# Second block of a two-block transformer: how the normalised rows get turned before each projection

## The chip, the core and the metric

One core of a Trainium2 chip runs the whole program in one launch. TensorE (PE) multiplies matrices into PSUM, VectorE (DVE), ScalarE (ACT) and GpSimd (POOL) work on SBUF and, but for POOL, on PSUM, and SyncE (SP) issues most DMAs. Each engine works off its own queue in order; they meet at semaphores. The metric is the device time of one execution in microseconds (us). Everything is float32.

## The reference, cut to what matters

Eight sequences of 512 rows of 256 numbers pass through two blocks, one after the other. The second block, which the change is about, does this for each sequence (16 heads of 64; context of 64 rows):

```
adaln(x, w, b) = ln(x) * w' + b'          # w', b': one vector of 256 per sequence
x = attn(adaln(x, 1), adaln(x, 1), sa) + x     # rotary self-attention, 512 x 512 scores
x = attn(adaln(x, 1), ln(context),  ca) + x     # rotary cross-attention, 512 x 64 scores
x = gelu(adaln(x, 2) @ ff_w1 + b1) @ ff_w2 + b2 + x     # hidden width 1024
```

`ln` subtracts a row's mean and divides by its standard deviation. The three `adaln` results feed the projections; a projection needs its input with the 256 features on partitions, while `ln` needs the rows on partitions. So 3 x 8 = 24 tiles of 512 x 256 have to be turned in this block.

## The kernel before, in words

**Tiles.** Each sequence's `x` stays in SBUF as a tile of 128 partitions x 4 x 256 (row t*128+p). A norm is made in three pieces (`norm_pieces`, lines 173-195): two of statistics, and `apply`, which writes the normed rows `z` with four DVE instructions (L191). `z` has one buffer in the pool `nk`, so the next sequence's `z` waits until this one has been read. POOL's `add_row` (L427) then adds an output bias to `x`.

**The turn.** `transposed` (lines 400-408) turns `z` with 8 PE transposes of 128 x 128 (L406) into two PSUM banks; ACT then writes the feature-major tile `hT`, scaled and shifted per feature (L407). `pair_turned` (lines 953-962) is the same in the self-attention stage, with one PSUM pair (L959, L961). `hT` has one buffer in each of the pools `nk` and `wk`.

**Stages.** Block 1 runs first (0 to about 804 us of the span). At its end `first_norm` and `first_turn` (lines 891-901) prepare the second block's first tile. Then follow self-attention (`slots`, to about 1758 us), cross-attention (`cross`, lines 1350-1393, to about 2093 us with the first feed-forward pieces in it) and feed-forward.

- Self-attention, per sequence four groups `g` of four heads. The next sequence's norm pieces stand in groups 0 and 1, its turn as the last job in the middle of group 2; group 3 makes its first queries, keys and values. `sums`, `sums_back`, `inverse` and `inverse_back` send the softmax sums through DRAM to spread them over partitions: den to DRAM, back as rec, reciprocal on DVE, to DRAM, back as `rb`, each broadcast to 64 partitions. The pool `wk` has two buffers with the tag `t`; the two rotary products and the values `v` for the next stage use them.
- Cross-attention, per sequence eight steps `j`. Queries run `LEAD` = 6 steps ahead, so sequence b+1 needs its `hT` at step j=2 of sequence b. Its rows are normed in the sequence before that, at j=5, 6 and 7 (`rows_`, `apply` at j=7, where it stands behind the residual addition of `cross_out`), and turned at j=1 (`turn`). The sums take the same way through DRAM: `sums` at j=0 (of the sequence before) and j=4, `inverse` at j=1 and j=6, with eight `rb` DMAs each.
- Feed-forward, per sequence `up` (f32 128 x 512 matmuls into hidden rows, gelu on ACT), the turn of the next sequence, and `down`, with the norm of the one after that in its middle.

**Order.** The order of instructions on PE, DVE, ACT and POOL is the program's own, by `manual_schedule` around each stage (lines 265, 1183, 1417). SP is not in these lists: the order of SP's DMAs is chosen by the tile framework's scheduler. All loads, the sums' DMAs and the output go by SP; the last sums of self-attention go by ACT's queue (`queue`, L1046). Waits on SP hold up all DMAs behind them.

Of the kernel before, what the change touches and what calls it, by code (L numbers as in the profile page):

```python
# [10 lines left out]
F32 = mybir.dt.float32  # L11
I32 = mybir.dt.int32
AF = mybir.ActivationFunctionType
ALU = mybir.AluOpType
AX = mybir.AxisListType
ENG = mybir.EngineType

B, N, D, H, T, CD, FF = 8, 512, 256, 16, 64, 192, 1024
P = 128
NT = N // P  # L20
EPS0, EPS1 = 1e-6, 1e-5
# [23 lines left out]
def fast_path(ctx: ExitStack, tc: tile.TileContext, a: dict, out: bass.AP):  # L45

    nc = tc.nc
# [4 lines left out]
    dram = ctx.enter_context(tc.tile_pool(name="dram", bufs=2, space=bass.MemoryType.DRAM))  # L52
# [10 lines left out]
    def pair():  # L63
        return psum.tile([P, 2, 512], F32, tag="pair", name="ps_P", bufs=4)
# [26 lines left out]
    ident = const.tile([P, P], F32, name="ident")  # L91
# [27 lines left out]
    def row(name):  # L119
        lo, hi = _ROWS[name]  # L120
        return rows[:, lo:hi]
# [27 lines left out]
    a1 = const.tile([P, 2, B], F32, name="a1")  # L149
    b1 = const.tile([P, 2, B], F32, name="b1")  # L150
# [59 lines left out]
    wk = sa0.enter_context(tc.tile_pool(name="sa0", bufs=2, side="right"))  # L210
# [51 lines left out]

    first_mod = bank_x()
    ms = ExitStack()
    ms.enter_context(tc.manual_schedule(engines={ENG.PE, ENG.DVE, ENG.Activation, ENG.Pool}))
    nc.sync.dma_start(cT, a["cT"].rearrange("(k p) b -> p k b", p=P))
    for k in range(2):
        nc.scalar.dma_start(adaw[:, k, 0 : 2 * D], a["adaln_wT"][k * P : (k + 1) * P, 0 : 2 * D])
# [131 lines left out]
    def transposed(pool, z, b, am, bm, bufs=2):  # L400

        hT = pool.tile([P, 2, N], F32, tag="hT", name="hT", bufs=bufs)
        for k in range(2):
            ps = bank_x()
            for t in range(NT):
                nc.tensor.transpose(ps[:, t * P : (t + 1) * P], z[:, t, k * P : (k + 1) * P], ident)  # L406
            nc.scalar.activation(hT[:, k, :], ps, AF.Identity, bias=bm[:, k, b : b + 1], scale=am[:, k, b : b + 1])  # L407
        return hT

    def normed_in_pieces(pool, b, eps, take):  # L410

        def rows_():
            z = pool.tile([P, NT, D], F32, tag="z", name="z", bufs=1)
            take(z)
            return z

        return norm_pieces(rows_, xs[b], eps)


    def normed(pool, b, eps):  # L420
        z = pool.tile([P, NT, D], F32, tag="z", name="z", bufs=1)
        layernorm(z, xs[b], eps)
        return z

    def add_row(b, r):

        nc.gpsimd.tensor_tensor(xs[b], xs[b], r[:, None, :].to_broadcast([P, NT, D]), ALU.add)  # L427
# [462 lines left out]

    def first_turn():
        nonlocal ready
        ready = transposed(nk, ready, 0, a1, b1, 1)

    def first_norm(n):
        nonlocal ready
        if n == 0:
            first.extend(normed_in_pieces(nk, 0, EPS1, first.append))
        first[n]()
        if n == 2:  # L900
            ready = first[-1]

    first = []
    beginning()
# [43 lines left out]
    with tc.tile_pool(name="ph4", bufs=2, reuse_waits="tile") as wk:  # L948
        NG = H // 4
        kb, vb = kv_first()  # L950
        first_rows, ahead = [], []

        def pair_turned(z, b):

            hT = nk.tile([P, 2, N], F32, tag="hT", name="hT", bufs=1)
            ps = pair()
            for k in range(2):
                for t in range(NT):
                    nc.tensor.transpose(ps[:, k, t * P : (t + 1) * P], z[:, t, k * P : (k + 1) * P], ident)  # L959
            for k in range(2):  # L960
                nc.scalar.activation(hT[:, k, :], ps[:, k, :], AF.Identity, bias=b1[:, k, b : b + 1], scale=a1[:, k, b : b + 1])  # L961
            return hT

        class Batch:

# [5 lines left out]
            def norm(self, n):  # L971
                self.pieces[n]()
                if n == 2:
                    add_row(self.b, row("sabo"))

            def turn(self):
                self.s["hT"] = pair_turned(self.s["z"], self.b)

            def values(self, half, t0):
                s = self.s  # L980
# [128 lines left out]
        def slots():  # L1109
            first = todo[0]  # L1110
            first.s["hT"] = ready
            second = pair()
            first.queries(0)
            add_row(0, row("sabo"))
            first.turned(0, w_sk, "k", second, nc.vector)
            first.values(0, 0)
            first.values(0, 2)
            before = None
            for b, this in enumerate(todo):
                nxt = todo[b + 1] if b + 1 < B else None  # L1120
                last = todo[b - 1] if b else None
                for g in range(NG):
                    for kt in range(2):
                        this.score(g, kt)
                    this.add(g, 1)
                    if g < NG - 1:
                        jobs = [lambda: this.queries(g + 1), lambda: this.keys(g + 1)]
                        if g == 1 and last:
                            jobs.append(last.out)
                        if b:  # L1130
                            jobs.append(lambda: this.values((g + 1) // 2, 2 * (1 - g % 2)))
                        elif g < 2:
                            jobs.append(lambda: this.values(1, 2 * g))
                        if g == 2 and nxt:
                            jobs.append(nxt.turn)
                    elif nxt:
                        jobs = [lambda: nxt.queries(0), lambda: nxt.keys(0), lambda: nxt.values(0, 0)]
                    else:
                        jobs = [lambda: cross_values(wk, 0)]
                    for n, fn in enumerate(jobs):  # L1140
                        fn()
                        if n == 0 and before:
                            before[0].inverse(before[1])
                        if n == 0 and nxt and g == 0:
                            nxt.norm(0)
                    if b == B - 1 and g == 2:
                        cross_weights()
                    if b == 0 and g == 1:
                        nc.gpsimd.memset(vb, 0.0)
                        load_kb(0)  # L1150
                    for kt in (2, 3):
                        this.score(g, kt)
                        this.add(g, kt)
                    this.value(g)
                    if nxt and g < 2:
                        nxt.norm(g + 1)
                    if before:
                        before[0].scaled(before[1])
                    this.sums(g)
                    before = this, g  # L1160
            end = todo[-1]
            first_rows.append(normed(nk, 0, EPS1))
            add_row(0, row("cabo"))
            cross_values(wk, 1)
            end.sums_back(NG - 1)
            cross_values(wk, 2)
            end.s["ps"] = [half[:, i, 0:D] for half in (pair(), pair()) for i in range(2)]
            end.inverse(NG - 1)
            cross_values(wk, 3)
            end.inverse_back(NG - 1)  # L1170
            load_vb(0)
            end.last_out(range(6))
            end.scaled(NG - 1)
            first_rows.append(pair_turned(first_rows[0], 0))
            end.last_out((6, 7))
            first_rows.append(normed(nk, 1, EPS1))
            add_row(1, row("cabo"))

            ahead.extend(normed_in_pieces(nk, 2, EPS1, lambda z: turned_rows.update({2: z})))
            ahead[0]()  # L1180
            ahead[1]()

        with tc.manual_schedule(engines={ENG.PE, ENG.DVE, ENG.Activation, ENG.Pool}):
            slots()
    other_banks()

    w_co, w_cq, ready = cross["o"], cross["q"], first_rows[1]
# [4 lines left out]
    with tc.tile_pool(name="ph5", bufs=2, reuse_waits="tile") as wk:  # L1192
# [3 lines left out]


        turned_rows = {0: ready, 1: first_rows[2]}

        pieces = {2: [lambda: None, lambda: None, ahead[2]]}  # L1200

        def rows_(i, n=None):

            if i < 2 * B:
                b = i % B
                if not n and i not in pieces:
                    pieces[i] = normed_in_pieces(nk, b, EPS1, lambda z: turned_rows.update({i: z}))
                for piece in pieces[i] if n is None else pieces[i][n : n + 1]:
                    piece()
                if n in (None, 2):  # L1210
                    add_row(b, row("ffb2" if i // B else "cabo"))

        def turn(i):
            if i < 2 * B:
                am, bm = ((a1, b1), (a2, b2))[i // B]
                turned_rows[i] = transposed((nk, wk)[i % 2], turned_rows[i], i % B, am, bm, 1)

        ss = [{} for _ in range(B)]

# [194 lines left out]
                    good = within(top)  # L1414
            return good

        with tc.manual_schedule(engines={ENG.PE, ENG.DVE, ENG.Activation, ENG.Pool}):
            cross()
            return feed_forward()

# [861 lines left out]
```

## Time and profile before

| | |
|---|---|
| runs | 2298.50, 2303.84, 2307.77 us, median 2303.84 |
| profiled execution | 2300.09 us, of which the span (first to last instruction) 2298.0 us |
| mean granted TensorE clock | 0.997 |
| all PE transposes of `transposed` (L406), 256 of them | 20.6 + 10.1 + 3.6 + 3.0 us busy |
| PE transposes of `pair_turned` (L959), 64 | 8.3 us busy |
| DMA engines | 10.7% of their time on SP's queue, 79 MB moved in all |

A timeline line reads: start in us of the span, length in us, engine, line of the kernel, operation, written tile <- read tiles, shapes, count of merged instructions; in brackets the idle time ahead of it and what ended that. A line of the chain of work reads: start, length, engine, tile written, line, count. Of a merged run of matmuls the length includes the last one's drain, so the next run starts a little before it ends. SP's lines show how long the issuing of a DMA took, not when it landed.

### The profile page before, as it was taken

What the parts mean: (1) busy time and instruction counts of PE and PEld (TensorE: products, weight loads), DVE (VectorE), ACT (ScalarE), POOL (GpSimd) and SP (SyncE); (2) the same over time, 40 slices, a digit from 0 to 9 for tenths busy, and PEclk for the clock granted to TensorE, in tenths of its full rate; (3) what the DMA queues carried; (4) which work ended last, traced back from release to release, by engine and by line L of the source; (5) the groups of instructions that cost most, each with busy time, mean ns of one, the idle gap of its engine ahead of it and who ended that gap; (6) DMA issues with size and microseconds to landing.
All of it is one profiled execution on the core that took longest, in us unless ns stands there. A gap on an engine that the chain in (4) does not pass through costs nothing.

```text
span 2298.0 us, 31044 instructions
## 1 busy us (share of the span) xinstructions
PE 2278.0 (99%) x12372; PEld 1169.5 (51%) x12372; DVE 1076.0 (47%) x1911; ACT 865.9 (38%) x1309; POOL 920.9 (40%) x584
## 2 busy tenths in 40 slices
PE   9999999999999999999999999999999999999999
PEld 4444554544545643535353444444445556567666
DVE  5676565565555345353444444444434554532110
ACT  5665555455542134342424333333332222231221
POOL 4653333333200046464545555554544544431110
PEclk9999999999999999999999999999999999999999
DMA  6120000000002000000000000000123222221000
GB/s 197 47 84 5 13 7 6 12 6 3 3 1 90 0 10 20 20 20 20 20 20 20 20 20 20 12 28 11 29 61 108 75 76 67 67 62 34 19 19 20
DMA packets 76697, 78.99 MB, mean 34 GB/s; under 512 B 37264, under 2 KB 54400, under 8 KB 76544
## 3 DMA queue, kind: packets, MB, share of 16 engines
q1 hardware_dynamic: 75064, 73.75, 10.7%
q8 instruction: 100, 1.64, 0.3%
q0 software_dynamic: 576, 2.10, 0.2%
q10 hardware_dynamic: 904, 1.07, 0.1%
q14 instruction: 53, 0.43, 0.1%
HBM read 67.38 MB, written 9.51 MB: 33 GB/s over the span
## 4 chain that ended last, share of the span: by engine, by line
PE 96%; DVE 2%; POOL 1%; issue 1%; ACT 0%; POOLq 0%; DVEq 0%; ACTq 0%
PE ps_P L88 41%; PE ps_B L88 30%; PE ps_X L88 7%; PE ps_S L88 6%; PE ps_D L88 5%; PE ps_O L88 4%; PE ps_B L545 1%; PE ps_B L406 1%; POOL var L536 1%; PE ps_B L577 1%; PE ps_X L406 0%; PE ps_P L959 0%; DVE z L191 0%; POOL rstd L158 0%; DVE st L182 0%
## 5 line engine op out<-in xcount | busy, mean ns | idle before, releaser
L594 ACT ACTIVATE p<-ps_B 128x512 f32<-128x512 f32 x576 | 292.6, 626 | 163.6 <-PE ps_B L88 163.5
L1020 ACT ACTIVATE p<-ps_P 128x1024 f32<-128x1024 f32 x256 | 245.1, 1027 | 95.1 <-PE ps_P L88 95.1
L88 PE MATMUL ps_P<-q,k 32*128 32x512 f32 x2048 | 239.1, 600 | 0.5 <-DVE t L999 0.5
L1029 POOL TENSOR_TENSOR sm<-sm,p 128x1024 f32<-128x1024 f32 x64 | 174.9, 2732 | 139.3 <-ACT p L1020 139.2
L88 PE MATMUL ps_B<-hT,w 128*128 128x512 f32 x512 | 226.6, 597 | 0.6 <-ACT hT L407 0.4
L88 PE MATMUL ps_P<-p,v 128*32 128x512 f32 x2048 | 226.4, 594 | 0.0
L158 POOL TENSOR_TENSOR rstd<-rstd,mhalf 128x4 f32<-128x4 f32 x49 | 52.0, 1062 | 325.7 <-DVE rstd L157 324.7
L988 ACT COPY v<-ps_P 128x1024 f32<-128x1024 f32 x32 | 32.4, 1013 | 377.0 <-PE ps_P L88 377.0
L1029 DVE TENSOR_TENSOR sm<-sm,p 128x1024 f32<-128x1024 f32 x64 | 98.5, 1538 | 150.3 <-ACT p L1020 150.3
L88 PEld LDWEIGHTS ps_P<-q,k 32*128 32x128 f32 x2048 | 101.1, 184 | 132.3 <-issue 104.5
L88 PEld LDWEIGHTS ps_B<-hT,w 128*128 128x128 f32 x512 | 95.4, 190 | 126.2 <-issue 99.9
L88 PEld LDWEIGHTS ps_P<-p,v 128*32 128x32 f32 x2048 | 63.3, 110 | 158.3 <-issue 134.8
L1027 POOL TENSOR_TENSOR sm<-p 128x1024 f32<-128x1024 f32 x32 | 79.2, 2474 | 160.6 <-ACT p L1020 160.6
L88 PE MATMUL ps_B<-q,k 16*128 16x512 f32 x1024 | 140.2, 617 | 1.4 <-DVE k L549 1.4
L536 POOL TENSOR_TENSOR var<-var,mhalf 128x32 f32<-128x32 f32 (+1 forms) x17 | 87.9, 5173 | 104.8 <-DVE var L530 104.8
L998 DVE TENSOR_TENSOR t<-ps_P,rope_c 128x1024 f32<-128x1024 f32 x64 | 78.4, 1225 | 107.9 <-POOL q L1002 66.2
L1027 DVE TENSOR_TENSOR sm<-p 128x1024 f32<-128x1024 f32 x32 | 39.2, 1226 | 185.7 <-ACT p L1020 185.7
L88 PE MATMUL ps_P<-hT,w_sa_wq 128*128 128x512 f32 x256 | 118.4, 605 | 0.8 <-DVE tmp L450 0.8
L88 PE MATMUL ps_B<-p,h 128*32 128x512 f32 x1024 | 117.1, 595 | 0.0
L588 POOL TENSOR_TENSOR attn<-attn,gate 128x256 f32<-128x256 f32 x32 | 23.6, 736 | 230.0 <-DVE attn L586 229.0
L88 PE MATMUL ps_B<-w,hid 128*128 128x256 f32 x512 | 115.4, 385 | 0.0
L88 PE MATMUL ps_P<-hT,w_sa_wk 128*128 128x512 f32 x256 | 115.1, 592 | 0.0
(260 smaller groups left out, 3716.5 us busy)
## 6 DMA issues: line engine op xcount, KB each, us to landing
rb<-rec SPq DMA_DIRECT2D x128, 128.0 KB
rb<-rec_d SPq DMA_DIRECT2D x124, 128.0 KB
out_dram<-x SPq DMA_DIRECT2D x15, 256.0 KB
x<-in_x_dram SPq DMA_DIRECT2D x7, 512.0 KB
gate<-modd SPq DMA_DIRECT2D x24, 128.0 KB
k_d<-q POOLq DMA_DIRECT2D x4, 512.0 KB, 4.0
v_d<-v SPq DMA_DIRECT2D x4, 512.0 KB
w_ff_w<-in_ff_w_dram SPq DMA_DIRECT2D x2, 1024.0 KB
```

The lines of the kernel that those rows point to most:

```text
L88: nc.tensor.matmul(o, lhsT, rhs, start=start, stop=stop)
L158: nc.gpsimd.tensor_tensor(r[:, :n], r[:, :n], mhalf[:, :n], ALU.pow)
L406: nc.tensor.transpose(ps[:, t * P : (t + 1) * P], z[:, t, k * P : (k + 1) * P], ident)
L536: nc.gpsimd.tensor_tensor(var, var, half, ALU.pow)
L545: nc.tensor.transpose(ps[:, t * P : (t + 1) * P], zs[c][:, t, lo : lo + P], ident)
L588: nc.gpsimd.tensor_tensor(attn, attn, gate.to_broadcast([P, NT, 4, HD0]), ALU.mult)
L594: nc.scalar.activation(p[i], ps, AF.Exp, scale=HD0 ** -0.5)
L988: nc.scalar.copy(s["v", half][:, t0 : t0 + 2, :], ps)
L998: nc.vector.tensor_tensor(c, ps, rope_c[:, None, :].to_broadcast([P, 2, N]), ALU.mult)
L1020: nc.scalar.activation(pr, pss[u], AF.Exp, scale=HD1 ** -0.5)
L1027: eng.tensor_tensor(s["sm", g, u], s["p", g, 0, u], s["p", g, 1, u], ALU.add)
L1029: eng.tensor_tensor(s["sm", g, u], s["sm", g, u], s["p", g, kt, u], ALU.add)
```

## The change

The second block's turns no longer use TensorE. DVE turns `z` in blocks of 32 x 32 (one instruction over 128 x 1024), four DMAs write the blocks to a DRAM tile in the order of the features, one DMA reads them back into the buffer of `z`, and ACT scales and shifts from SBUF into `hT`. The DMAs and the block-turn are issued right after `apply`, ahead of `add_row`; ACT's instructions stand where the turn stood. In the self-attention stage the block-turned copy takes a buffer of the tag `t`; elsewhere it takes the coming `hT` tile itself. SP joins the engines in program order, in all three stages. Block 1's turns stay as they were.

```diff
+    def blocks_turned(by_way, z):
+
+        flat_, zf = by_way.rearrange("p k n -> p (k n)"), z.rearrange("p t d -> p (t d)")
+        nc.vector.transpose(flat_.rearrange("p (q t i) -> p t q i", q=8, t=NT), z.rearrange("p t (q j) -> p t q j", j=32))
+        d = dram.tile([4, 32, 2, 4, P], F32, tag="turned", name="turned_d")
+        for r in range(4):
+            nc.sync.dma_start(d[:, :, :, r, :].rearrange("a j k c -> j k a c"),
+                              flat_[32 * r : 32 * r + 32].rearrange("j (k a c) -> j k a c", k=2, a=4))
+        nc.sync.dma_start(zf, d.rearrange("a j k r c -> (a j) (k r c)"))
+        return zf.rearrange("p (k r t i) -> p k t r i", k=2, r=4, t=NT)
+
+    def modulated(hT, raw, b, am, bm):
+
+        for k in range(2):
+            nc.scalar.activation(hT[:, k, :].rearrange("p (t r i) -> p t r i", t=NT, r=4), raw[:, k], AF.Identity,
+                                 bias=bm[:, k, b : b + 1], scale=am[:, k, b : b + 1])
+        return hT
...
     def first_turn():
         nonlocal ready
-        ready = transposed(nk, ready, 0, a1, b1, 1)
+        ready = modulated(first[-1], ready, 0, a1, b1)
...
         if n == 2:
-            ready = first[-1]
+            z = first[-1]
+            first.append(rows_tile(nk))
+            ready = blocks_turned(first[-1], z)
...
                 if n == 2:
+                    self.s["raw"] = blocks_turned(by_way(), self.s["z"])
                     add_row(self.b, row("sabo"))
 
             def turn(self):
-                self.s["hT"] = pair_turned(self.s["z"], self.b)
+                self.s["hT"] = modulated(rows_tile(nk), self.s["raw"], self.b, a1, b1)
...
-            first_rows.append(normed(nk, 0, EPS1))
+            first_rows.append(blocks_turned(by_way(), normed(nk, 0, EPS1)))
             add_row(0, row("cabo"))
...
-            first_rows.append(pair_turned(first_rows[0], 0))
+            first_rows.append(modulated(rows_tile(nk), first_rows[0], 0, a1, b1))
             end.last_out((6, 7))
-            first_rows.append(normed(nk, 1, EPS1))
+            first_rows.append(blocks_turned(by_way(), normed(nk, 1, EPS1)))
...
                 if n in (None, 2):
+                    row_tiles[i] = rows_tile((nk, wk)[i % 2])
+                    turned_rows[i] = blocks_turned(row_tiles[i], turned_rows[i])
                     add_row(b, row("ffb2" if i // B else "cabo"))
...
-                turned_rows[i] = transposed((nk, wk)[i % 2], turned_rows[i], i % B, am, bm, 1)
+                turned_rows[i] = modulated(row_tiles.pop(i), turned_rows[i], i % B, am, bm)
...
-        with tc.manual_schedule(engines={ENG.PE, ENG.DVE, ENG.Activation, ENG.Pool}):
+        with tc.manual_schedule(engines={ENG.PE, ENG.DVE, ENG.Activation, ENG.Pool, ENG.SP}):
```

`rows_tile(pool)` allocates a tile `hT` as before, and `by_way()` a tile `t` of the self-attention stage. The last hunk stands for three places: ENG.SP is added to each `manual_schedule`. The four outgoing DMAs carry 128 KB each in runs of 512 bytes, the one back 512 KB in runs of 4 KB.

More of the change, by code (lines that the diff above doesn't have):

```diff
@@ L264, in fast_path @@
     ms = ExitStack()
-    ms.enter_context(tc.manual_schedule(engines={ENG.PE, ENG.DVE, ENG.Activation, ENG.Pool}))
+    ms.enter_context(tc.manual_schedule(engines={ENG.PE, ENG.DVE, ENG.Activation, ENG.Pool, ENG.SP}))
     nc.sync.dma_start(cT, a["cT"].rearrange("(k p) b -> p k b", p=P))
@@ L407, in transposed, with rows_tile @@
             nc.scalar.activation(hT[:, k, :], ps, AF.Identity, bias=bm[:, k, b : b + 1], scale=am[:, k, b : b + 1])
+        return hT
[8 more added lines that the diff above has]
+        return zf.rearrange("p (k r t i) -> p k t r i", k=2, r=4, t=NT)
+    def rows_tile(pool, bufs=1):
+        return pool.tile([P, 2, N], F32, tag="hT", name="hT", bufs=bufs)
+    def modulated(hT, raw, b, am, bm):
+        for k in range(2):
+            nc.scalar.activation(hT[:, k, :].rearrange("p (t r i) -> p t r i", t=NT, r=4), raw[:, k], AF.Identity,
+                                 bias=bm[:, k, b : b + 1], scale=am[:, k, b : b + 1])
         return hT
@@ L951, in fast_path, with by_way @@
         first_rows, ahead = [], []
[L953 to L962, printed above, removed]
+        def by_way():
+            return wk.tile([P, 2, N], F32, tag="t", name="t")
         class Batch:
@@ L1198, in fast_path @@
         turned_rows = {0: ready, 1: first_rows[2]}
+        row_tiles = {1: rows_tile(wk)}
         pieces = {2: [lambda: None, lambda: None, ahead[2]]}
@@ L1415, in feed_forward @@
             return good
-        with tc.manual_schedule(engines={ENG.PE, ENG.DVE, ENG.Activation, ENG.Pool}):
+        with tc.manual_schedule(engines={ENG.PE, ENG.DVE, ENG.Activation, ENG.Pool, ENG.SP}):
             cross()
```

## The prediction

> **What bounds the kernel now.** I read the page's busy times first, then the chain of work in order of time, stage by stage.
>
> ```profile
> PE 2278.0 (99%) x12372; PEld 1169.5 (51%) x12372; DVE 1076.0 (47%) x1911; ACT 865.9 (38%) x1309; POOL 920.9 (40%) x584
> PE 96%; DVE 2%; POOL 1%; issue 1%; ACT 0%; POOLq 0%; DVEq 0%; ACTq 0%
> ```
>
> TensorE is busy 99% of the span and is 96% of the chain. So what leaves PE is won, and what makes PE wait is lost, one for one. Two pieces of the chain show the price of a turn, one from self-attention, one from feed-forward:
>
> ```profile
> 1350.96 0.87 PE ps_P L959 x8
> 1351.84 116.42 PE ps_P L88 x704
> 1468.26 0.87 PE ps_P L959 x8
> ```
>
> ```profile
> 2236.36 13.73 PE ps_S L88 x32
> 2250.09 0.87 PE ps_X L406 x8
> 2250.97 6.91 PE ps_D L88 x32
> ```
>
> Eight transposes take 0.87 us, and nothing but PE stands in the chain on either side: a sequence of self-attention is 116.42 + 0.87 = 117.29 us.
>
> **What goes.** 24 turns of 0.87 us. Self-attention has seven of them in its chain (sequences 1 to 7): 6.1 us. Cross-attention has eight (tiles 1 to 8): 7.0. Feed-forward has seven (9 to 15): 6.1. The first turn, at the end of block 1, also ends an idle gap of 0.96 us in which PE waits for DVE's z: 1.8 together. The turn of tile 0 at the end of self-attention (1754.07) I count at nothing: right behind it PE needs products that POOL ends at 1754.12 (1752.85 + 1.27, waiting for rb), so a gain would only meet that wait. Sum: 21.0 us.
>
> **What comes: the way from z to hT.** Before, hT needed PE and ACT. Now it needs DVE's block-turn, four DMA issues, their landing, a fifth DMA that waits for them, its landing, and ACT. The trace shows none of this for these shapes; each step is bounded by near rows.
>
> - Block-turn, 128 x 1024 f32: DVE's L1027 of the same size takes 1.23; the four apply instructions of the same data take 1.38 alone and 3.30 beside POOL. 1.2 to 3.4; I take 1.25, since add_row, POOL's next work, starts only after apply and the row of one DVE pass is the nearest.
> - Issues: SP takes 0.32 for rec and 4.96 / 8 = 0.62 for an rb. Four: 1.3 to 2.5. I take 0.6 each, as for rb, which like these writes is no plain block: 2.4.
> - Landing of the last write: den issued at 1012.20 for 0.52, rec, which waits for it, at 1013.90: 1.2 for 8 KB. The slow end are the rb reads below: 2.4 for 128 KB. I take 1.6.
> - Way back, 512 KB: issue 0.3 to 0.6, taken 0.5. Landing 2.5 (the 1.2 above plus 512 KB at the 388 GB/s of the weight loads between 730 and 740 us) to 3.4 (an rb plus the same rate for three times 128 KB more); taken 3.0.
> - ACT's first half, 0.78 now from PSUM, 0.60 for the tanh of the same size: taken 0.78.
>
> ```profile
> 2065.76 4.92 SPq L1285 DMA_DIRECT2D rb<-rec  x8
> ```
>
> ```profile
> 2073.01 0.74 DVE L1292 TENSOR_TENSOR p<-p,rb 128x512 f32<-128x512 f32 x1 [1.54 <-DMA rb<-rec]
> ```
>
> The last of the eight rb was issued by 2070.68, its reader starts at 2073.01: 2.3 to 2.5 for all four readers of this kind.
>
> Sum: 1.25 + 2.4 + 1.6 + 0.5 + 3.0 + 0.78 = **9.5 us**, between 7.0 and 13.1.
>
> [...]
>
> **Where that way is hidden.** In self-attention z ends at 1101.65 and ACT comes to hT at 1117.33: 15.7 us, so the way is covered with 6 to spare. By_way holds one of two t buffers until the four writes have landed (about 1107); the second rope product that could need it starts at 1110.76. The sums' den DMA (1102.97) now queues behind the way back until about 1107.5 and rec gets to DVE at about 1112 to 1113, where DVE takes it at 1111.89 now and then idles 2.2 us: covered. In feed-forward z ends at 2120.7 and ACT ends its gelus at 2137.5: covered. At the first turn PE's eight banks hold four ups of 3.45 us, so ACT, held until 771 (z at 760.97), has until about 774.
>
> **Where it is not hidden: cross-attention.**
>
> ```profile
> 1863.09 7.07 PE L88 MATMUL ps_O<-vw,p 128*128 128x256 f32 x32
> 1870.09 1.06 PE L88 MATMUL ps_X<-p,sel 128*32 128x512 f32 x8
> ...
> 1876.53 1.04 PE L406 MATMUL ps_X<-ident,z 128*128 128x128 f32 x8
> ...
> 1880.85 1.88 PE L88 MATMUL ps_X<-hT,w_ca_wq 128*128 128x512 f32 x4
> ```
>
> ```profile
> 1870.80 1.38 DVE L191 TENSOR_SCALAR z<-x,mv,rstd 128x256 f32<-128x256 f32 x4
> ```
>
> z waits on DVE behind the residual of the last cross_out of a sequence (PE until 1870.1) and ends at 1872.18. PE needs hT at 1880.85, without the transposes at 1879.98: 7.8 us later. The way takes 9.5, so PE waits 1.7 us. Tiles 3 to 8 repeat this, as z hangs on PE's own j=7: 6 x 1.7 = 10.2 us (none to 6 x 5.3 by the bounds). Tile 2 is worse: z ends at 1799.03, and SP is issuing rb until about 1800.7, so the first write goes out at 1800.8 and hT comes at 1809.1, where PE wants it at 1803.85: 5.2 us.
>
> What queues behind: ACT holds only copies whose banks PE takes up later than j=2; on DVE, the reciprocal of the second half waits for rec, whose den now follows the fifth DMA.
>
> **The clock.** Gaps also cost granted clock. The rows differ: a gap of 1.36 us before 144.46 was followed by 3.4 us at half clock (1.7 lost), one of 1.10 before 1769.68 by none, one of 3.77 before 691.29 by 6.4 us (3.2 lost).
>
> ```profile
> 143.00:144.00 1.00, 0.10 (x1) 0.00 (x0) 0.96 (x2) 1.00 (x3) 0.00 (x0) 1.00 1.01 418
> 144.00:145.00 1.00, 0.54 (x2) 0.46 (x3) 1.00 (x3) 1.00 (x3) 0.00 (x0) 0.86 1.01 414
> 145.00:146.00 1.00, 1.00 (x4) 0.82 (x3) 1.00 (x3) 0.73 (x2) 0.00 (x0) 0.50 0.31 111
> ```
>
> The last figures but two are the clock: 1.00, 0.86, 0.50. For tile 2 I add 3.2; for the six gaps of 1.7 us, between the row that fell and those that did not, half of them: 3 x 1.7 = 5.1 (0 to 10.2).
>
> [...]
>
> **The rest.** At the start of cross-attention PE idles 0.30 and 1.10 us on DVE's rope products (1767.45, 1769.68); the block-turn of tile 1 stands ahead of them: +1.25. In the last sums of self-attention v's buffers and the rb issue move by about 3 us on ACT, while the weight loads that delayed rb (landed 1751.2) now follow in program order: zero, -1 to +2. SP in program order in block 1 moves loads that are early anyway: nothing; if one came late, it would show as PE idle there.
>
> **Sum.** -21.0 + 10.2 + 5.2 + 3.2 + 5.1 + 1.25 = +4.0 us on the profiled 2300.1, thus 2304. That execution lies 3.8 under the median of the runs, so for the median 2303.8 + 4.0 = **2308**.
>
> **Rivals.**
>
> *The way is short enough* (faster). If it takes at most 7.8 us from z to hT, the six gaps vanish; by the low ends only tile 2 is late, 2.7 plus 1.7 clock. -21.0 + 4.4 + 1.25 = -15.3: 2288. For it: 512-byte writes may drain while SP still issues, and 0.33 us issues exist. Against: all three low ends at once.
>
> *The way is longer and the clock falls with every gap* (slower). At 11.5 us, midway to the upper bound, each gap is 3.7, as long as the row of 3.77, and costs 3.2 more: 6 x 6.9 + 7.2 + 3.2 + 1.25 - 21.0 = +32: 2336. It decides from gaps somewhere between 1.4 and 3.8 us. For it: DVE beside POOL, writes to DRAM read right back. Against: the landings of 1.2.
>
> *SP's order takes the place of the wait* (slower). den goes out at 1878 and not at 1871.88, rec and the eight rb follow; cross_out wants the last scaled tile at about 1894.6. I get 1892.9, since vb (2.02 us) no longer stands ahead of rb. If den behind 512 KB costs 3 us more, each of seven sequences loses 1.3: 2317.
>
> *The change does not give PE back what it removes*: in self-attention ACT's exponentials, 0.43 us behind hT, take the place of the transposes. Then 6.1 is not won: 2314.
>
> **How the numbers follow.** A measurement of this kernel tells about 0.5% from no change: faster is below 2292.3, slower above 2315.4. Forecast 0.38 (own range 2298 to 2315), short way 0.24, long way 0.26, SP's order 0.07, no gain 0.05. Faster 0.24; same 0.38 + 0.05 = 0.43; slower 0.26 + 0.07 = 0.33. The range takes in both ways: 2286 to 2338.
>
> **What would show it.** L406 keeps 128 transposes, L959 goes. Self-attention's period falls to 116.4, feed-forward's 28.42 to 27.55. In cross-attention PE's wait ahead of the first query of each tile, put down to ACT's hT, is about 1.7 us, and ACT's to the DMA of z. [...] PE idle on DVE's reciprocal or on rb at j=5 shows SP's order. I am wrong altogether if self-attention shows new waits on t or rec.

## The result

The changed kernel takes **2322.77 us** (median of 4 runs, 2319.84 to 2323.46), the kernel before beside it 2301.17 (2298.17 to 2307.77): ratio **1.0087**, 95% interval [1.0061, 1.0114]. It is slower by 21.6 us, above the forecast of 2308 and inside the range. The profiled execution took 2323.46 us, its span is 2321.6, its granted clock 0.989 (before: 2300.09, 2298.0, 0.997).

The page of the kernel after first: busy times, and the shares of the chain of work.

```profile
PE 2274.8 (98%) x12180; PEld 1153.6 (50%) x12180; DVE 1113.9 (48%) x1935; ACT 864.8 (37%) x1309; POOL 922.6 (40%) x584
...
PE 91%; DVE 3%; DMA 3%; POOL 1%; issue 1%; SPq 1%; ACT 0%; ACTq 0%; DVEq 0%; POOLq 0%
```

192 matmul instructions are gone, as promised (24 turns of 8). But PE's busy time falls only by 3.2 us, because more of what is left runs at half clock (mean 0.989, before 0.997), and PE is now 91% of the chain instead of 96%: DVE, DMA and SP's issues stand in it.

Where the time went, by marks that both traces have (the first self-attention product, the first cross-attention query, the first `up`, the end):

| stage | before | after | predicted | measured |
|---|---|---|---|---|
| block 1 and first turn | 803.85 | 804.45 | -1.8 | +0.6 |
| self-attention | 954.55 | 953.92 | -6.1 | -0.6 |
| cross-attention | 274.72 | 303.95 | +18.0 | +29.2 |
| feed-forward | 264.88 | 259.28 | -6.1 | -5.6 |
| sum | | | +4.0 | +23.6 |

The last sum is the difference of the two profiled spans; the medians differ by 21.6.

Two pieces of the chain of work of the kernel after, in order of time (start, length, engine, tile, line, count):

```profile
884.50 847.48 PE ps_P L88 x5164
...
2232.86 13.73 PE ps_S L88 x32
2246.60 6.91 PE ps_D L88 x32
2253.50 6.91 PE ps_O L88 x32
```

The turns are really out of PE's way here: one unbroken piece of self-attention without an L959, and in feed-forward no L406 between `up` and `down`. Seven tiles of feed-forward give 5.6 of the 6.1 us. What PE waits for from the end of self-attention on is in the list of waits (waiter, awaited, us in total, times, longest):

```profile
PE ps_X L88 <- ACT hT L427: 20.1, 6, 6.3
PE ps_O L88 <- DVE t L847: 4.2, 1, 4.2
PE ps_S L88 <- ACT hT L427: 2.3, 1, 2.3
PE ps_P L88 <- DVE oT L1103: 2.1, 1, 2.1
PE ps_P L88 <- POOL oT L1103: 1.6, 1, 1.6
```

Line one and three are the gaps ahead of the first use of hT for tiles 2 to 8 (6.28 for tile 2; 2.69, 2.59, 2.84, 3.01, 2.64 and 2.31 for tiles 3 to 8). Line two is the start of cross-attention, the last two are the end of self-attention. Before, the same list (from 1740 us on) held rope products and nothing else:

```profile
PE ps_D L88 <- DVE t L826: 1.1, 1, 1.1
PE ps_X L88 <- DVE t L826: 0.3, 1, 0.3
```

**The way from z to hT**, for one tile (timeline of the kernel after, other lines left out):

```profile
1886.80 1.38 DVE L191 TENSOR_SCALAR z<-x,mv,rstd 128x256 f32<-128x256 f32 x4
...
1888.21 1.25 DVE L413 STREAM_TRANSPOSE hT<-z 128x1024 f32<-128x1024 f32 x1
...
1889.49 2.61 SPq L416 DMA_DIRECT2D turned_d<-hT  x4
...
1894.19 0.33 SPq L418 DMA_DIRECT2D z<-turned_d  x1
...
1897.87 1.52 ACT L427 ACTIVATE hT<-z,b,a 128x512 f32<-128x512 f32 x2 [4.55 <-DMA z<-turned_d]
...
1898.73 1.55 PE L88 MATMUL ps_X<-hT,w_ca_wq 128*128 128x512 f32 x3 [2.59 <-ACT hT L427]
```

From z's end (1886.80 + 1.38 = 1888.18) to PE's query at 1898.73 are 10.55 us: 1.25 for the block-turn, 4.7 until the four writes have landed, 3.5 for the way back (issue and landing; 3.49 in the chain of work), 0.9 for ACT's first half, the rest handing over. PE would have come 7.8 us after z: that is its slack. Behind three of the six gaps of tiles 3 to 8 the first query takes 3.42 to 3.50 us and not 1.98: half clock, some 1.5 us each.

**The end of self-attention** (timeline of the kernel after):

```profile
1738.12 1.01 ACT L966 COPY v<-ps_P 128x1024 f32<-128x1024 f32 x1 [5.11 <-DMA turned_d<-t]
...
1738.53 0.94 SPq L967 DMA_DIRECT2D v_d<-v  x2
...
1744.26 1.01 ACT L966 COPY v<-ps_P 128x1024 f32<-128x1024 f32 x1 [5.13 <-DMA v_d<-v]
1744.28 3.02 ACTq L1097 DMA_DIRECT2D rb<-rec_d  x4
...
1750.52 0.69 DVE L1103 TENSOR_TENSOR oT<-oT,rb 128x512 f32<-128x512 f32 x1 [16.15 <-DMA rb<-rec_d]
```

The same place before: ACT's copy waits for PE alone.

```profile
1743.95 1.01 ACT L943 COPY v<-ps_P 128x1024 f32<-128x1024 f32 x1 [2.46 <-PE ps_P L88]
1744.03 2.46 ACTq L1081 DMA_DIRECT2D rb<-rec_d  x4
```

ACT issues the last rb behind these copies of v. In both kernels that happens about 940 us after self-attention's first product (1744.03 and 1744.28), although after the change PE comes here 5.6 us earlier (ACT's first v copy starts 933.2 us after that product before, 927.6 after). What seven sequences won is lost here in one place.

### The profile page after: what moved, and what is told of

The parts are those of the page before. It is cut to its first block, busy times and chain, and to the rows that moved or that the text cites. A ratio compares the mean times of both kernels' runs of the same rounds, so it can differ in the third digit from the quotient of the medians.

```text
span 2321.6 us, 30915 instructions
## 1 busy us (share of the span) xinstructions
PE 2274.8 (98%) x12180; PEld 1153.6 (50%) x12180; DVE 1113.9 (48%) x1935; ACT 864.8 (37%) x1309; POOL 922.6 (40%) x584
## 4 chain that ended last, share of the span: by engine, by line
PE 91%; DVE 3%; DMA 3%; POOL 1%; issue 1%; SPq 1%; ACT 0%; ACTq 0%; DVEq 0%; POOLq 0%
PE ps_P L88 40%; PE ps_B L88 30%; PE ps_X L88 7%; PE ps_S L88 5%; PE ps_D L88 4%; PE ps_O L88 2%; DMA z<-turned_d 1%; DMA turned_d<-hT 1%; PE ps_B L566 1%; DVE z L191 1%; SPq L416 1%; PE ps_B L406 1%; POOL var L557 1%; PE ps_B L598 1%; DVE hT L413 0%
## 5 line engine op out<-in xcount | busy, mean ns | idle before, releaser
L88 PE MATMUL ps_P<-w_sa_wo,oT 128*128 128x256 f32 x512 | 114.0, 383 | 3.7 <-DVE oT L1103 2.1
```

What stands on the lines that cost most here:

```text
L88: nc.tensor.matmul(o, lhsT, rhs, start=start, stop=stop)
```

## The experiments

Each ratio is to runs of the kernel before on the same chip (medians 2302.91 beside e1 to e4, 2300.01 beside e5 to e8, 2299.39 beside e9 to e11), so runs of different series are compared by it.

| run | us | ratio, 95% interval |
|---|---|---|
| e1, SyncE's order alone | 2300.68 | 0.9998 [0.9987, 1.0009] |
| e2, the turning alone | 2322.70 | 1.0090 [1.0071, 1.0109] |
| e3, tiles 2 to 8 turned by PE | 2295.36 | 0.9968 [0.9957, 0.9978] |
| e4, cross-attention's turns earlier | 2295.71 | 0.9972 [0.9959, 0.9985] |
| e5, e4 + another buffer for tile 0 | 2297.26 | 0.9985 [0.9975, 0.9995] |
| e6, e4 + tile 1's turn later | 2292.80 | 0.9964 [0.9950, 0.9978] |
| e7, every turn under cover | 2283.53 | 0.9921 [0.9907, 0.9936] |
| e8, writes on two queues | 2319.13 | 1.0083 [1.0067, 1.0098] |
| e9, writes as whole rows | 2309.29 | 1.0042 [1.0027, 1.0057] |
| e10, one write | 2300.58 | 0.9996 [0.9986, 1.0005] |
| e11, e7 + tile 1's norm earlier | 2280.58 | 0.9911 [0.9897, 0.9926] |

### Which half of the change costs: e1 and e2

e1 is the kernel before with this in all three places; e2 is the kernel after with it taken back:

```diff
-tc.manual_schedule(engines={ENG.PE, ENG.DVE, ENG.Activation, ENG.Pool})
+tc.manual_schedule(engines={ENG.PE, ENG.DVE, ENG.Activation, ENG.Pool, ENG.SP})
```

> The kernel before, with SyncE in program order in the three hand-ordered stretches and nothing turned by VectorE. First theory (the way from z to hT in cross-attention is longer than PE's slack, and its gaps cost clock; SyncE's order costs nothing): as before, ratio 0.999 to 1.002, cross-attention's period stays 38.06 us, the last sums of self-attention end as before. Rival (SyncE's order is itself the cost, as rec and rb come later behind other issues): 5 to 20 us slower, with PE idle on rb or on DVE's reciprocal. Of the 4.4 us that the profile after is late by in the first 100 us, this run tells too: if they are SyncE's order they are here again.

> The kernel after, with SyncE left to the scheduler again: only the turning is changed. First theory: about as after, ratio 1.006 to 1.011, with gaps of about 2.6 us ahead of the first query of cross-attention's tiles and a period near 41 us. Rival (SyncE's order): near before, ratio 0.995 to 1.002, period 37.2 to 38.1 us. If the first products of cross-attention stand between tile 1's norm pieces again on DVE, the 5.5 us lost at that start come from SyncE's order, else from the turn.

Measured: 0.9998 and 1.0090. e1's cross-attention takes 274.72 us, to the hundredth what it takes before; e2 has the same gaps as after (cross-attention 302.58) and the same 4.15 us at its start. So SyncE's order costs nothing by itself, and the 5.5 us at the start of cross-attention come with the turn. The few us by which the profile after is late in its first 100 us were no cost of the change either: the first self-attention product comes at 803.85 before, 807.10 in e1 and 800.75 in e6, whose block 1 is the same as after's, so a single profile says nothing of +-3 us there.

### Is it the way in cross-attention: e3 and e4

In e3, in `rows_` and `turn`:

```diff
-                    row_tiles[i] = rows_tile((nk, wk)[i % 2])
-                    turned_rows[i] = blocks_turned(row_tiles[i], turned_rows[i])
+                    if not 2 <= i <= B:
+                        row_tiles[i] = rows_tile((nk, wk)[i % 2])
+                        turned_rows[i] = blocks_turned(row_tiles[i], turned_rows[i])
...
+                if 2 <= i <= B:
+                    turned_rows[i] = transposed((nk, wk)[i % 2], turned_rows[i], i % B, am, bm, 1)
...
```

In e4, in `cross`:

```diff
-                    if j > 4:
-                        rows_(b + 2, j - 5)
+                    if 1 < j < 5:
+                        rows_(b + 2, j - 2)
```

> The kernel after, but tiles 2 to 8 (cross-attention's 2 to 7 and feed-forward's first) are turned by PE again; tile 0, tile 1, self-attention and the other seven of feed-forward stay as changed. First theory: the gaps go and the period is 38.06 us again: 24 to 26 us less than after, about 2297, ratio 0.997 to 1.000 to before (won: 12 in self-attention and feed-forward, lost again: about 5 at the end of self-attention, about 5 at the start of cross-attention). Rival (the loss lies in the end of self-attention and in SyncE's order): 2310 to 2320, as taking the way out of cross-attention would give back little.

> The kernel after, but in cross-attention the norm of tile b+2 and its turn stand at j = 2, 3, 4 and no longer at j = 5, 6, 7, so that the way from z to hT has some 17 us more before PE wants hT. First theory: no gap ahead of the first query, period 37.2 us (38.06 less the 0.87 of the transposes): 6 x 4 + 7 = about 30 us less than after, 2290 to 2298, ratio 0.995 to 0.999 to before. Rival (the loss is not the length of the way but that five more DMAs stand ahead of rec and rb on SyncE's queue, or that VectorE's turn holds DVE): the gaps move to rb or to the reciprocal and the time stays over 2310.

Both win back 27 us against the 2322.7 of e2 and of the kernel after: 2295.4 and 2295.7. In e4 no wait on hT is left and two sequences take 74.38 us (60.97 + 13.41 between the marks of their scores), 37.19 each: the 38.06 of before less the 0.87 of the transposes. The rival is out. One part of it was seen all the same, at one place. e4's waits of PE from 1740 us on, but for the two at the end of self-attention (2.2 and 1.7 us, as in the kernel after):

```profile
PE ps_D L88 <- DVE t L847: 4.3, 1, 4.3
PE ps_O L88 <- DVE t L847: 4.2, 1, 4.2
...
```

The second is the start of cross-attention, as in after. The first is new (at 1815.01): in sequence 0 the turn of tile 2 now stands ahead of rec and rb on SyncE, DVE's scaled products wait 5.05 and 1.79 us for rb, rope products stand behind them, and PE waits; half clock follows. That cost e4 some 6 us (an estimate: the wait and 1.7 us of clock).

### The two ends: e5, e6, e7, e11

e5, on top of e4 (the modulated copy goes into the same tile):

```diff
-            first_rows.append(blocks_turned(by_way(), normed(nk, 0, EPS1)))
+            first_tile = rows_tile(nk)
+            first_rows.append(blocks_turned(first_tile, normed(nk, 0, EPS1)))
```

> The kernel with cross-attention's turns at j = 2, 3, 4 (2295.7), and tile 0's block-turn, at the end of self-attention, writes into the free hT tile in place of a t buffer. If the t buffer that the four writes hold is what delays v, rec and rb there, ACT's wait of 5.1 us on the writes goes, DVE's oT comes 4 to 5 us earlier than 1750 and the time is about 2291 (ratio 0.995). Rival: SyncE's queue is what delays, as the stores of v stand behind the way back of z, which waits for the writes; then ACT's second wait (5.1 us on a store of v) stays or grows, and at most 2 us are won: 2294 to 2296.

A miss for my theory, and the rival's case in its mechanism; in time 2297.26 lies above both bands. ACT and SP in e5:

```profile
1738.62 0.33 SPq L418 DMA_DIRECT2D z<-turned_d  x1
1738.99 0.91 SPq L967 DMA_DIRECT2D v_d<-v  x2
...
1745.21 1.01 ACT L966 COPY v<-ps_P 128x1024 f32<-128x1024 f32 x1 [8.29 <-DMA v_d<-v]
```

The wait on the t buffer is gone, and the next wait is longer by 3.2 us: the stores of v stand on SyncE behind the way back of z, which waits for the writes. Self-attention takes 954.20 us, e4's 954.13. So in this order of SyncE it is the queue that holds ACT, and not the buffer.

The queue isn't the whole of it. In e2, where the scheduler orders SyncE, ACT waits 0.24 us for the stores of v, and the last rb goes out 937.5 us after self-attention's first product and not 939.8:

```profile
1741.02 3.39 ACTq L1097 DMA_DIRECT2D rb<-rec_d  x4
...
1751.97 0.69 DVE L1103 TENSOR_TENSOR oT<-oT,rb 128x512 f32<-128x512 f32 x1 [18.59 <-DMA rb<-rec_d]
```

Yet e2's self-attention takes 955.11 us: DVE has rb 10.95 us after the first issue, and 6.24 in the kernel after. From 1739 to 1749 us the 16 DMA engines are busy for at least 0.89 of the time in e2 and in the kernel after, with v and the weights of feed-forward; that rb has to share them with these is argued, not tested.

e6, on top of e4:

```diff
-            first_rows.append(blocks_turned(by_way(), normed(nk, 1, EPS1)))
+            first_rows.append(normed(nk, 1, EPS1))
...
                 queries(n)
+                if n == 0:
+                    turned_rows[1] = blocks_turned(row_tiles[1], turned_rows[1])
```

> The kernel with cross-attention's turns at j = 2, 3, 4 (2295.7), and tile 1's turn written behind the first query of cross-attention and no longer at the end of self-attention, so that DVE takes the first rope products between the norm's pieces, as before the change. If DVE's order at that start is what costs about 5.5 us there (4.2 us idle and half clock behind it), the wait of 4.2 us shrinks to 1 to 2.5 us and the time falls by 2 to 5 us, to 2291 to 2294 (ratio 0.995 to 0.996). Rival: PE waits there for something else (v's loads, POOL's q): the time stays at 2295 to 2297.

Two lines of the kernel after show what was to be tested: in order, DVE takes tile 1's whole norm, its block-turn (1764.21) and tile 2's statistics, and only then the first rope products.

```profile
1767.28 0.68 DVE L846 TENSOR_TENSOR t<-ps_O,rope_c 128x512 f32<-128x512 f32 x1
...
1768.70 2.05 PE L88 MATMUL ps_O<-w_ca_wo,kv 128*128 128x256 f32 x4 [4.15 <-DVE t L847]
```

Before, this product stood ahead of the norm's `apply`:

```profile
1761.41 0.69 DVE L825 TENSOR_TENSOR t<-ps_O,rope_c 128x512 f32<-128x512 f32 x1
...
1763.32 1.38 DVE L170 TENSOR_SCALAR z<-x,mv,rstd 128x256 f32<-128x256 f32 x4 [0.54 <-POOL rstd L158]
```

In e6 it does so again (1758.34); the wait of 4.15 becomes 1.44 and 1.09, without half clock, and cross-attention falls from e4's 280.26 to 276.78. The ratios of e4 and e6 (0.9972 and 0.9964) are too near to tell them apart; the stage's length is what shows it.

e7, on top of e6, puts every turn where its way is covered:

```diff
-            first_rows.append(blocks_turned(by_way(), normed(nk, 0, EPS1)))
-            add_row(0, row("cabo"))
...
                     if nxt and g < 2:
                         nxt.norm(g + 1)
+                    if not nxt and g == 1:
+                        first_rows.append(blocks_turned(by_way(), normed(nk, 0, EPS1)))
+                        add_row(0, row("cabo"))
...
+                    if b == 0 and j == 2:
+                        rows_(2, 2)
-                    if 1 < j < 5:
+                    if b and 1 < j < 5:
                         rows_(b + 2, j - 2)
```

> Every turn placed where its way is covered: cross-attention's at j = 2, 3, 4, tile 2's at j = 2 of sequence 0 (ahead of the first den and rec on SyncE), tile 1's behind the first query, tile 0's norm and turn inside the last batch of self-attention. First theory (removing 0.87 us a turn is worth its full price and all the loss is ways that aren't covered): the 21 us of the removed turns remain less 1 to 3 us at the start of cross-attention: 2282 to 2287, ratio 0.991 to 0.9935 to before. Rival (half of the loss is something else, clock in block 1 or DMA traffic): 2289 to 2295.

2283.53, ratio 0.9921: inside the first theory's band. Self-attention takes 949.49 us (954.55 before, 953.92 after), so 5.1 of the 6.1 us of its seven turns arrive, and cross-attention 271.94.

e11, on top of e7, moves tile 1's norm too, and with it hT of tile 0 (the lines stood at the end of the stage):

```diff
             end.sums_back(NG - 1)
+            first_rows.append(modulated(rows_tile(nk), first_rows[0], 0, a1, b1))
             cross_values(wk, 2)
...
             end.inverse(NG - 1)
+            first_rows.append(normed(nk, 1, EPS1))
+            add_row(1, row("cabo"))
+
+            ahead.extend(normed_in_pieces(nk, 2, EPS1, lambda z: turned_rows.update({2: z})))
+            ahead[0]()
+            ahead[1]()
```

> The run with every turn placed where its way is covered (2283.5), with tile 1's norm and the statistics of tile 2 moved from the start of cross-attention into DVE's wait for rb at the end of self-attention (DVE idles 11.8 us there). If DVE's order is what still makes PE wait at the start of cross-attention (1.44 and 1.10 us on rope products), both gaps go and the time falls by 2 to 3 us: 2280 to 2282, ratio 0.9895 to 0.992 to before. Rival: rb comes later as the normed rows wait for ACT, or POOL's add of a row delays its product: 2283 to 2287.

2280.58, ratio 0.9911: the fastest here, 18.8 us under the kernel before. All that PE still waits for from 1740 us on in e11:

```profile
PE ps_D L88 <- DVE t L847: 2.2, 1, 2.2
PE ps_P L88 <- POOL oT L1103: 1.0, 1, 1.0
```

Cross-attention falls from 271.94 to 268.46 against e7; by the ratios alone the two can't be told apart.

### What the way is made of: e8, e9, e10

All three are the kernel after, changed for tiles 2 to 8 only.

e8, in `blocks_turned` (`late` is true for these tiles):

```diff
-            nc.sync.dma_start(d[:, :, :, r, :].rearrange("a j k c -> j k a c"),
+            (nc.scalar if late and r > 1 else nc.sync).dma_start(d[:, :, :, r, :].rearrange("a j k c -> j k a c"),
```

> The kernel after, with two of a turn's four writes issued by ACT and two by SyncE for tiles 2 to 8 (the way is shorter by two issues of 0.65 us, nothing moves). First theory: the gap ahead of the first query falls one for one, from about 2.6 to 1.3 us, and the period from 41.1 to 39 to 39.8 us: 8 to 13 us less than after, 2309 to 2315, ratio 1.003 to 1.006. If the granted clock still falls after every second gap of 1.3 us, 2315; if such gaps are too short for that, 2309 or less. Rival: the gap is set by the landing of the writes and not by their issue, or ACT loses what SyncE wins: 2320 to 2324.

2319.13: the rival's case, all but 1 us; both of its halves are seen. SP and ACT issue side by side (1.54 and 1.26 us), yet the writes have landed 4.07 us behind the first issue and not 4.7; the gaps are 1.83 to 2.30. The DMA engines of the kernel after suggest why (columns: busy us of PE, PEld, DVE, ACT, POOL, then granted clock, share of the 16 DMA engines, GB/s):

```profile
1891.00:1892.00 1.00, 1.00 (x6) 0.87 (x5) 0.99 (x2) 0.21 (x2) 1.00 (x2) 1.00 0.98 180
1892.00:1893.00 1.00, 1.00 (x6) 0.68 (x5) 1.00 (x2) 0.72 (x2) 1.00 (x1) 1.00 1.00 205
```

While the writes run, all 16 engines are busy, at 180 to 205 GB/s; on the way back they reach 344 in the same profile. So issuing 1.1 us faster brought the landing only 0.6 us forward. And ACT lost some of it: in sequence 0 its two issues stand ahead of a copy of den, for which PE waits 1.94 us.

e9, in `blocks_turned` (`d` is the DRAM tile); in e10 both 32 are 128, so that there is one write. Both leave out the move between the blocks, so their rows come back in the wrong order:

```diff
+            dw = d.rearrange("a j k r c -> (a j) (k r c)")
+            for lo in range(0, P, 32):
+                nc.sync.dma_start(dw[lo : lo + 32], flat_[lo : lo + 32])
+            nc.sync.dma_start(zf, dw)
```

> The kernel after, but for tiles 2 to 8 the four writes go to DRAM as whole rows of 4 KB a partition, not in pieces of 512 bytes, so that those tiles' blocks of 32 come back in the wrong order (this leaves out the move between the blocks; bytes and number of DMAs stay). If the pieces set the landing (the 16 engines are busy 0.98 to 1.00 at 180 to 205 GB/s while the writes run, and move 344 on the way back), the landing falls from 4.6 us behind the first issue to about 3.3 and the gap of 2.6 us to about 1.3: period near 39.2, time 2309 to 2314. If the four issues set it, nothing changes: 2320 to 2324.

> As the run with whole rows, but one write of 512 KB in place of four of 128 KB (again without the move between the blocks). If issues and pieces together make the way, it falls by 1.9 us more (three issues of 0.65) and the gaps go, or are under 0.5 us: period 37.2 to 37.8 for tiles 3 to 8, time 2298 to 2303 (the two losses at the ends of self-attention and at tile 2 remain). If the trip to DRAM and back costs a fixed 5 us or more whatever its shape, a gap over 1 us stays and the time is 2308 or more.

Both came as forecast in time: 2309.29 and 2300.58. In e9 the four issues take less, too:

```profile
1886.12 1.73 SPq L418 DMA_DIRECT2D turned_d<-hT  x4
1889.73 0.34 SPq L419 DMA_DIRECT2D z<-turned_d  x1
...
1894.31 1.98 PE L88 MATMUL ps_X<-hT,w_ca_wq 128*128 128x512 f32 x4 [1.54 <-ACT hT L433]
```

Issue to landing falls from 4.7 to 3.6 us, the gaps to 1.36 to 1.85, the period (one sequence) to 39.0 to 39.3. With one write it is 2.6 us, and tiles 3 to 7 wait 0.6 on average; the period, 38.1 to 38.2, is a little longer than forecast. So the pieces of 512 bytes cost about 1.1 us of each way (0.9 of it in the issues) and the three extra DMAs another 1.0: of the 10.55 us some 2 are the shape of the writes. What is left, 8.4 us, is a trip of the same bytes without the move between blocks, and still over PE's slack of 7.8.

## Why the prediction was right or wrong

Right in sign of most terms and in mechanism, wrong in size at three places. The likeliest case (2308) failed; the time lies half way to "the way is longer and the clock falls with every gap" (2336), but by other terms. It is above 2315.4, the prediction's own bound for "slower", to which it had given 0.33.

- **What goes.** The periods of self-attention and feed-forward fell by the 0.87 a turn that was foretold (e4's cross-attention, 37.19, the same). The 1.8 of the first turn is won, too (2.7 and 3.1), but only profiles whose clock fell at the same places in block 1 show it: it takes 807.10 us in e1 and 804.45 in the kernel after, 803.85 before and 800.75 in e6. That the kernel after is 0.6 us later than before, 2.4 off the forecast, is where the clock fell in these two executions (last section), and not the turn. In the first sequence of self-attention a wait on a rope product grew from 0.46 to 1.36 us: 0.9 lost, which no term had.
- **The end of self-attention, "zero, -1 to +2": the worst step.** It lost 5.0 us: the lead of 5.6 with which PE came to it is 0.6 at its end. The prediction named v's buffers and the rb issue, but let them slip by 3 us against a rb that it held to be delayed by the weight loads anyway. In fact the stores of v wait on SP behind the way back of z, ACT's copies wait for them, and the last rb goes out 5 to 6 us later than it could. e5 shows that it is the queue and not the buffer, e2 that rb can come late without it, e7 that the loss goes when the turn is moved away. "Which queue is it moved past" had been asked of den, and not of v.
- **The start of cross-attention, "+1.25": 5.5.** Counted was the block-turn alone. What changed was that the whole norm of tile 1 stood ahead of the rope products, and the gap of 4.15 cost clock; in e6 and e11, which undo that order, the loss goes. Why the scheduler no longer took the two stages' work in turns when the block-turn stood at their seam is not shown.
- **The way, 9.5: 10.55.** Block-turn (1.25) and way back (3.5) are exact (the low end of the sum, given as 7.0, adds up to 7.1). The writes' issue was 2.6 for 2.4 and their landing 2.0 behind the last issue for 1.6; ACT and the handing over made another 0.4. Against a slack of 7.8 an error of a tenth in the way is one of six tenths in the gap: 2.31 to 3.01 of idle time and not 1.7. Between the starts of the queries each gap costs 0.27 more than the idle time shows: tile 4's query starts 41.52 us behind tile 3's, and 41.52 - 37.19 (the period) - 1.48 (tile 3's half clock) = 2.85, where the idle time is 2.59. That makes 17.7 us for the six and not 10.2: +7.5.
- **The clock, half of the six gaps by 1.7:** three fell, by 1.44 to 1.52 each. The number is right by luck: half was taken because the rows of before differed, and the gaps were longer than the 1.7 us it was taken for. e9 has six gaps of 1.36 to 1.85 us, and the clock fell behind none of them.
- **Tile 2, 5.2 + 3.2:** a gap of 6.28 and half clock behind it; 8.6 in all between the starts of matmuls (6.4 + 2.1 of clock), for 8.4. Right.
- **SP's order, the rival at 2317:** refuted by the list of waits, where PE waits for no rb and no reciprocal in cross-attention, and by e2, which has the same gaps in the scheduler's order. e1 (0.9998) shows that the order without the turns costs nothing. It cost only where a turn's DMAs stood ahead of others that were due: v's stores at the end of self-attention, and rec in e4's sequence 0.

Added up, these terms make the 19.6 us between the two sums: 5.5 (self-attention) + 4.2 (start of cross-attention) + 7.5 (gaps) - 0.7 (their clock) + 0.2 (tile 2) + 2.4 (block 1) + 0.5 (feed-forward).

## What to carry to other kernels

Work taken off the bounding engine and sent by way of DRAM was worth its full price here only where the whole way was covered (e4: 38.06 to 37.19 us a sequence of cross-attention, against 40.1 to 42.0 in the kernel after). One and the same edit was 21.6 us slower where the old order stood, and about 18.8 us faster than before once every norm was made early enough, so move the producer first. No run moves the norms and keeps the old turn; as PE waited for only 1.4 us from 1740 us on before, that alone could win little there. For a DMA that waits, look not only at what it feeds but at every store and load behind it on its queue, up to those whose buffers another engine is waiting for (v, then rb: 5.0 us lost at the end of self-attention). And a slack is a difference of two long times, so price the way to a tenth before trusting a gap of 1.7 us.

## What the runs showed of the hardware

**When the clock falls.** The gap of 2.69 us before 1857.21 was followed by half clock, the longer one of 3.01 before 1981.02 was not. Read in windows of 0.1 us, the falls of a profile lie on one grid of 3.4133 us (after: 577 steps from the fall at 51.15 us to that at 2020.64, and all drops between at 3.36 to 3.38 modulo that; e8: all at 0.24 to 0.26), and half clock lasts 3.41 or 6.83 us in the kernel after. Where the grid lies differs from one execution to the next (1.36 in the profile before). The windows of that grid around two gaps of the kernel after (first figure behind the length: PE busy; last but two: clock):

```profile
1853.40:1856.81 3.41, 1.12 (x6) 0.64 (x4) 0.72 (x2) 0.46 (x1) 2.48 (x2) 1.00 0.53 163
1856.81:1860.22 3.41, 3.01 (x4) 1.46 (x5) 0.63 (x3) 2.01 (x4) 0.00 (x0) 0.50 0.06 10
1894.36:1897.77 3.41, 1.78 (x9) 1.22 (x7) 1.29 (x2) 0.00 (x0) 1.88 (x2) 1.00 0.50 159
1897.77:1901.19 3.42, 2.46 (x6) 1.25 (x7) 1.06 (x4) 2.47 (x4) 0.60 (x1) 1.00 0.08 14
```

In the first window PE idles 3.41 - 1.12 = 2.29 us, and the next one runs at half clock; the second gap is cut in two by the grid, 1.63 and 0.96, and the clock stays at 1.00. In the profiles of the kernel after, e8 and the kernel before, up to 2273 us and leaving out windows with the matmuls of the next paragraph, the 13 windows with 2.17 us or more of idle time (7, 5 and 1) were all followed by half clock (as in the first row), and none of the 12 from 0.93 to 1.68 (5, 5 and 2); from 1.81 to 1.94 there were both. That also fits e9, whose gaps of 1.36 to 1.85 in cross-attention cost no clock at all (its periods are all 39.0 to 39.3 us).

Not every fall follows idle time. Three falls of the kernel after, at 51, 82 and 102 us, follow windows in which PE is busy for all of 3.41 us, but for 2.84 to 2.99 us of it with scores of block 1 that use 16 partitions (16x512). A fourth, at 140 us, follows one with 2.70 us of them and 0.32 of idle time, and the fall behind a gap of 1.36 us at 144.72 us in the kernel before follows one with 1.17 us of them. Whether such matmuls bring the falls is not shown: no run here was made to test it, and the window of the kernel after that starts at 54.56 us has 2.68 us of them and was not followed by half clock. Before's grid has no window with more than 2.42 us of them in this stretch. Three falls of 1.7 us each are about the 4.4 us by which the profile after was late at that place. e1, which turns everything on PE as before, has the same three falls (807.10 us to the first self-attention product), and e6, whose block 1 is the changed one, has none of them (800.75): so they were no cost of the change.

**DMA writes in pieces.** Four writes of 128 KB in pieces of 512 bytes took 0.65 us each to issue (2.61 for the four in the kernel after), and while they ran the 16 DMA engines were busy 0.98 to 1.00 of the time at 180 to 205 GB/s; as rows of 4 KB they took 0.43 each (1.73 in e9).
